# Layer 0 query projection as seven block products, rotated block by block, with the modulation weights loaded in halves

## The chip, the core and the metric

The kernel runs on one core of a Trainium2 chip. A core has five engines with a queue each: TensorE (PE; its weight loads are listed apart as PEld), VectorE (DVE), ScalarE (ACT), GpSimd (POOL) and SyncE (SP), which issues the DMA transfers. An engine works its own queue off in order and waits for the others at semaphores. The metric is the device time of one execution in microseconds (us), the median of several runs.

## The reference

Two transformer layers over x of 2 batches x 512 tokens x 512 features, all in fp32. Each layer has a modulated layer norm, attention, and a feed-forward part. The change touches only the attention of layer 0 and the products that make the modulation vectors:

```python
mod = (_silu(L0_c) @ L0_wmod).reshape(L0_c.shape[0], 6, 1, -1)   # 512 x 3072 weights, 2 rows
sa, ca, ga, sb, cb, gb = (mod[:, 0], mod[:, 1], ..., mod[:, 5])
h = _layernorm(x, axis=-1) * (1 + ca) + sa
# attention of layer 0: 32 query heads of 128, 8 key/value heads, window of 128 tokens
q = (x @ wq).reshape(B, S, 32, 128)      # x is h here; wq is 512 x 4096
k = (x @ wk).reshape(B, S, 8, 128)
v = (x @ wv).reshape(B, S, 8, 128)
q = _rope(q, pos); k = _rope(k, pos)     # [t1*cos - t2*sin, t1*sin + t2*cos] over the head's two halves
scores = einsum('bqhgd,bshd->bhgqs', qg, k) * 128 ** -0.5
allowed = (j <= i) & (j > i - 128)
attn = softmax(where(allowed, scores, min), axis=-1)
out = einsum('bhgqs,bshd->bqhgd', attn, v).reshape(B, S, 4096)
x = x + ga * (out @ wo)
```

## The kernel before

**Units and steps.** Layer 0's attention (`attention0`) works in 16 units: unit u is one key/value head (a group of 4 query heads) with one batch, the two batches of a group one after the other, so that even units bring in a new group of weights. A unit has four steps, one for each block `qb` of 128 queries; step n = 4u + qb. All tiles are transposed: features on the 128 partitions, tokens along the free dimension. The loop (under `tc.manual_schedule`, L965) writes out by hand the order in which PE, DVE, ACT and POOL get their instructions: the order of the program text is the order of each engine's queue. SP's order is set by a scheduler.

In step n of unit u, with `new` = u + 1, the text has in this order:

- `scores(u, qb)`: 4 or 8 small products into the one score tile in PSUM (`sp`, a single buffer), then on DVE the band mask (L809) and the row maximum (L815).
- The projections of the next unit: `keys(new)` and head 0 of the queries at qb 0, `values(new)` and head 1 at qb 1, heads 2 and 3 at qb 2 and 3.
- `turned`: the transposes of the step before (L844), their copies by ACT and DVE (L846).
- `exponentials` (ACT, reading `sp`; L825) and `normalised` (DVE reciprocal L834, POOL multiply L835).
- `product(u - 1, ...)`: the output projection of the unit before. It already is a seven-product (Strassen) form: each product is 4 matmuls of 256 columns (L903), added by DVE into sums that stay in SBUF (L911). The order is 1,2 / 7,4 / 5,6 / 3 over the four steps.
- `mix`: probabilities times values (L855), copied out by DVE (L862).
- `combine_rows` (L884, four POOL operations after the last `mix` of a unit), `combine_group` (L696, four POOL operations at the end of an even unit), and pieces of the modulation (`aside`).

**The query projection before.** `queries(u, hh)` calls `roped` (L736) for one head: 4 matmuls of 512 columns (the 512 features in 4 chunks, L740; the trace shows each fp32 matmul as two records) into one PSUM tile, then the rotation: three DVE multiplications that read that PSUM tile and the cosine/sine table (L745, L748, L749), and one POOL addition into `qT` (L750). All four heads of a unit are finished within the four steps before the unit's own first step.

**Buffers.** The PSUM pool `pmm` has four buffers, which keys, queries, values, products and mixes use in turn. The probabilities `p` have three buffers.

**Modulation.** Ten of the twelve 512 x 512 blocks of the modulation weights come in during the attention, in five pairs: a step issues the pair's two loads of 1 MB (`loads`, L558), the next one does its 8 matmuls (`mod_rows`, L99), the next turns the rows into columns or gates, and one pair has a `spread` step. The first pair (for the first norm) is loaded at the start.

**Feed-forward weights.** `Ffn0.loads` puts W and the low-rank matrices into the two buffers that the modulation weights used, from step 20 on.

Of the kernel before, what the change touches and what calls it, by code (L numbers as in the profile page):

```python
# [45 lines left out]
def adaln_kernel(ctx: ExitStack, tc: tile.TileContext, A: dict, out: bass.AP):  # L46
# [23 lines left out]
    def load_wmod(L, pool, bufs):  # L70

        src = A[f"L{L}_wmod"].rearrange("(kc p) n -> p kc n", p=P)

        def load(s):
            w = pool.tile([P, KC, D], F32, tag="wmod", name=f"wmod{L}_{s}", bufs=bufs)
            nc.sync.dma_start(out=w, in_=src[:, :, s * D : (s + 1) * D])
            return w

        return load
# [19 lines left out]
    def mod_rows(L, ws, sc, pool, tmp):  # L99

        n = 32 * len(ws)
        which = "".join(str(s) for s in ws)
        ps = pool.tile([P, 512], F32, tag="mm", name=f"psr{L}_{which}")
        for kc in range(KC):
            for i, w in enumerate(ws.values()):
                nc.tensor.matmul(
                    ps[32 * i : 32 * (i + 1), :],
                    lhsT=sc[:, kc, :],
                    rhs=w[:, kc, :],
                    start=(kc == 0),  # L110
                    stop=(kc == KC - 1),
                )
        rows = tmp.tile([P, D], F32, tag="rows", name=f"rows{L}_{which}", bufs=2)
        nc.scalar.copy(rows[:n, :], ps[:n, :])
        return rows
# [94 lines left out]
    class Ffn0:  # L210
# [3 lines left out]
        def __init__(self, gate, mid, wmp, ap, psum):  # L214
            self.gate, self.mid, self.wmp, self.ap, self.psum = gate, mid, wmp, ap, psum

        def loads(self):
            self.wT = self.wmp.tile([P, KC, D], F32, tag="wmod", name="wT0", bufs=2)
            nc.sync.dma_start(out=self.wT, in_=A["L0_ffn_WT"].rearrange("(kc p) o -> p kc o", p=P))

            self.ab = self.wmp.tile([P, KC, D], F32, tag="wmod", name="abT0", bufs=2)
            nc.sync.dma_start(
                out=self.ab[:, :, : 2 * P], in_=A["L0_ffn_AT"].rearrange("(kc p) e -> p kc e", p=P)
            )
            for j in range(2):
                nc.sync.dma_start(
                    out=self.ab[:, 2 * j : 2 * j + 2, 2 * P :],
                    in_=A["L0_ffn_BT"][j * P : (j + 1) * P, :].rearrange("p (h o) -> p h o", h=2),
                )
            co = self.mid.tile([P, 2, 2], F32, tag="co", name="co0")  # L230
            for i, n in enumerate(("L0_ffn_coeffs", "L0_ffn_scales")):
                for j in range(2):
                    src = A[n][j * 8 : (j + 1) * 8].unsqueeze(1).to_broadcast([8, R]).unsqueeze(2)
                    nc.sync.dma_start(out=co[:, i, j : j + 1], in_=src)
            self.wrow = self.mid.tile([P, 2], F32, tag="wrow", name="wrow0")
            nc.vector.tensor_mul(self.wrow, co[:, 0, :], co[:, 1, :])
# [30 lines left out]
        def tile(self, t):  # L267
            b, cols = t // TB, bass.ts(t % TB, P)
            ps = self.psum.tile([P, 512], F32, tag="mm", name=f"psf0_{t}")
            for kc in range(KC):  # L270
                nc.tensor.matmul(  # L271
                    ps, lhsT=hT[b][:, kc, cols], rhs=self.wT[:, kc, :], start=(kc == 0), stop=False
                )
            for j in range(2):
                nc.tensor.matmul(
                    ps.rearrange("p (h o) -> p h o", h=2),
                    lhsT=self.xa[:, 2 * b + j, cols],
                    rhs=self.ab[:, 2 * j : 2 * j + 2, 2 * P :],
                    start=False,
                    stop=(j == 1),  # L280
                )
            y = self.ap.tile([P, D], F32, tag="y", name=f"yf0_{t}", bufs=2)
            nc.vector.tensor_mul(y, ps, self.gate[b])
            nc.gpsimd.tensor_add(xs[t], xs[t], y)
# [247 lines left out]
    with ExitStack() as c01:  # L532
# [7 lines left out]
        with ExitStack() as c00:  # L540
            tables, load_group, combine_group = weights0(tc, A, c00)
            wmp = c00.enter_context(tc.tile_pool(name="wm", bufs=1))
            load = [load_wmod(L, wmp, 2) for L in range(2)]
            w = {s: load[0](s) for s in (0, 1)}
            load_x()
            tabs, groups = tables(), [load_group(0)]
            with ExitStack() as c0:
                pmm = c0.enter_context(tc.tile_pool(name="pmm0", bufs=3, space=PSUM))
                mod_columns(0, w, mod_rows(0, w, scs[0], pmm, wmp), pmm)
                norm = Norm(0, 0, 1, mid)  # L550
                for b in range(B):
                    norm.batch(b, pmm)

            def modulation(L, pair, pool):
# [3 lines left out]
                def loads():  # L558
                    held["w"] = {s: load[L](s) for s in pair}

                def rows():
                    held["r"] = mod_rows(L, held["w"], scs[L], pool, wmp)

                def rest():
                    if pair == (2, 5):
                        gate_rows(L, pair, held["r"], wmp, grow[L])
                    else:
                        mod_columns(L, pair, held["r"], pool)
# [4 lines left out]
                return [loads, rows, rest] + ([spread] if pair == (2, 5) and L == 0 else [])  # L573

            def finale(ap, pool):

                f = Ffn0(gate[5], mid, wmp, ap, pool)
                n0 = Norm(0, 3, 4, mid)
                end = (NKV * B - 2) * TB
                steps = {20: [f.loads]}  # L580
# [5 lines left out]
                steps[end + 5].insert(0, f.bias)  # L586

# [34 lines left out]
            def reload(t):  # L622
# [5 lines left out]
                tc, small, hT, xs, X, reload, gate[2], ident, tabs, groups, load_group,  # L628
                combine_group,
                lambda pool: [  # L630
                    f
                    for L, pair in ((0, (2, 5)), (0, (3, 4)), (1, (0, 1)), (1, (3, 4)), (1, (2, 5)))
                    for f in modulation(L, pair, pool)
# [21 lines left out]
def weights0(tc, A, ctx):  # L655
# [19 lines left out]
    def load_group(g):  # L675
# [7 lines left out]
        nc.sync.dma_start(out=w["q"], in_=wq[:, :, g * QW : (g + 1) * QW])  # L683
        for k in range(2):
# [10 lines left out]

    def combine_group(g, w):  # L696
# [9 lines left out]
    return tables, load_group, combine_group  # L706


def attention0(
    tc, small, hT, xs, X, reload, ga, ident, tabs, groups, load_group, combine_group, aside, finale  # L710
# [12 lines left out]
    with ExitStack() as ctx:  # L723
# [5 lines left out]
        kTs, vs, qTs, oTs, nms, pes, pTs, s3s, olds = ({} for _ in range(9))  # L729
# [6 lines left out]
        def roped(dst, wcols, b, name):  # L736

            ps = pmm.tile([P, 512], F32, tag="mm", name=f"ps_{name}")
            for kc in range(KC):
                nc.tensor.matmul(  # L740
                    ps, lhsT=wcols(kc), rhs=hT[b][:, kc, :], start=(kc == 0), stop=(kc == KC - 1)
                )
            co, si = rope[:, 0, :], rope[:, 1, :]
            t1 = ap.tile([P, S], F32, tag="t1", name=f"t1_{name}")
            nc.vector.tensor_mul(t1, ps, co)  # L745
            t2 = ap.tile([P, S], F32, tag="t2", name=f"t2_{name}")
            h = HD // 2
            nc.vector.tensor_mul(t2[:h, :], ps[h:, :], si[h:, :])  # L748
            nc.vector.tensor_mul(t2[h:, :], ps[:h, :], si[:h, :])  # L749
            nc.gpsimd.tensor_add(dst, t1, t2)  # L750

        def keys(u):
            g, b = units[u]
            kTs[u] = ap.tile([P, S], F32, tag="kT", name=f"kT{u}")
            roped(kTs[u], lambda kc: groups[g]["k"][:, kc, :], b, f"k{u}")
# [16 lines left out]
        def queries(u, hh):  # L772
            g, b = units[u]
            if hh == 0:
                qTs[u] = ap.tile([P, GRP, S], F32, tag="qT", name=f"qT{u}")
            roped(
                qTs[u][:, hh, :],
                lambda kc: groups[g]["q"][:, kc, hh * HD : (hh + 1) * HD],
                b, f"q{u}_{hh}",
            )  # L780

# [4 lines left out]
        def scores(u, qb):  # L786
# [4 lines left out]
            for hh in range(GRP) if qb == 0 else ():  # L791
                nc.tensor.matmul(
                    sp[:, hh, o:],
                    lhsT=qTs[u][:, hh, :P],
# [4 lines left out]
            for hh in range(GRP) if qb else ():  # L799
                for h in range(2):  # L800
# [3 lines left out]
                        lhsT=qTs[u][:, hh, qb * P + h * H2 : qb * P + (h + 1) * H2],  # L804
# [13 lines left out]
        def exponentials(u, qb):  # L818
# [3 lines left out]
            pe = ap.tile([P, GRP, 2 * P], F32, tag="p", name=f"p{u}_{qb}", bufs=3)  # L822
# [61 lines left out]
        def combine_rows(u):  # L884

            a11, a12, a21, a22 = quarters(u)
            s3 = s3s[u] = ap.tile([P, 2, DH], F32, tag="s3", name=f"s3_{u}", bufs=1)
            nc.gpsimd.tensor_sub(s3, a11, a21)
            nc.gpsimd.tensor_add(a21, a21, a22)
            nc.gpsimd.tensor_sub(a11, a21, a11)  # L890
            nc.gpsimd.tensor_sub(a12, a12, a11)
# [45 lines left out]
        def output(u, i):  # L937
# [12 lines left out]
            y = ap.tile([P, D], F32, tag="y", name=f"ya{u}_{i}", bufs=2)  # L950
# [3 lines left out]
        aside = aside(pmm)  # L954
# [10 lines left out]
        with tc.manual_schedule(engines=FOUR):  # L965
            for n in range(-TB, NU * TB + 2):
# [6 lines left out]
                if new < NU:  # L973
                    if qb == 0:
                        keys(new)
                        queries(new, 0)
                    elif qb == 1:
                        values(new)
                        queries(new, 1)
                    else:  # L980
                        queries(new, qb)
# [8 lines left out]
                if 0 <= u - 1 < plain:  # L990
                    for i in ((1, 2), (7, 4), (5, 6), (3,))[qb]:
                        product(u - 1, i)
                if 0 <= n - 1 < NU * TB:
                    mix(*before)
                    if before[1] == TB - 1 and before[0] < plain:
                        combine_rows(before[0])
                for f in filling.get(n, ()):
                    f()
                if 0 <= u < plain and qb == TB - 1 and units[u][1] == 0:
                    combine_group(units[u][0], groups[units[u][0]])  # L1000
                for f in regaining.get(n, ()):
# [792 lines left out]
```

## Time and profile before

Three runs took 2500.97 us (median), 2496.91 and 2504.66. The profiled execution took 2495.89 us; its span, from first to last instruction, is 2494.0 us. The rest, 1.9 us, lies around the span.

| what | value |
|---|---|
| span of the profiled execution | 2494.0 us |
| time of the profiled execution | 2495.89 us |
| median of three runs | 2500.97 us |
| PE busy, whole span | 2425.6 us (97%) |
| attention of layer 0, unit 0's first scores to the last group's end | about 60 to 845 us of the span |
| one unit in the steady part (scores of qb 0 to the next scores of qb 0) | 545.06 to 592.80 us: 47.74 us |
| mean granted TensorE clock over the span | 0.985 |

Two notes for reading. In a timeline row the columns are: start, time from the first instruction's start to the last one's end, engine, line, operation, out<-in, partitions x elements, count, and in brackets the idle time of the engine before it and what ended it. PE's instructions are pipelined and their ends are modelled, so the time that a set of matmuls costs is read from its start to the start of the next set.

### The profile page before, as it was taken

The numbers are of one execution on the slowest core, as the hardware profiler recorded it, in microseconds if no ns is written. First come the engines' busy times: TensorE is split into PE (matmuls) and PEld (weight loads), VectorE is DVE, ScalarE is ACT, GpSimd is POOL, SyncE is SP. The second block draws the span as 40 slices with busy tenths as digits, with TensorE's granted clock in tenths as the row PEclk, the third lists the DMA queues.
The fourth block names the chain that finished last, engine by engine and source line by source line (L and its number), as shares of the span: only waits on it lengthen the run. The fifth ranks groups of instructions, "written<-read, shape, count | busy, mean of one in ns | idle before, by whom it ended". The sixth has DMA issues, their size and how long they took to land.

```text
span 2494.0 us, 30184 instructions
## 1 busy us (share of the span) xinstructions
PE 2425.6 (97%) x11036; PEld 1196.2 (48%) x11036; DVE 1719.7 (69%) x2352; ACT 1411.4 (57%) x2106; POOL 1634.9 (66%) x1563
## 2 busy tenths in 40 slices
PE   7999999999999999999999999999999999999878
PEld 3566666666666544444444344444344444444333
DVE  4546666655667436788777788778777877788764
ACT  1222212212222116888888888878788888888650
POOL 1434444344356414888888988889888888888743
PEclk8999999999999999999999999999999999999988
DMA  6221100100000101000000000000000000110000
GB/s 231 79 74 60 43 14 30 41 15 30 13 6 29 32 15 34 26 26 19 25 26 26 22 26 26 26 26 18 30 26 26 26 18 26 30 29 22 18 9 34
DMA packets 74559, 83.06 MB, mean 33 GB/s; under 512 B 7725, under 2 KB 58700, under 8 KB 74412
## 3 DMA queue, kind: packets, MB, share of 16 engines
q1 hardware_dynamic: 74268, 81.00, 10.3%
q8 instruction: 87, 1.43, 0.2%
q14 instruction: 60, 0.49, 0.1%
q0 software_dynamic: 144, 0.15, 0.0%
HBM read 79.03 MB, written 2.10 MB: 33 GB/s over the span
## 4 chain that ended last, share of the span: by engine, by line
PE 94%; DVE 4%; ACT 1%; DMA 0%; issue 0%; POOL 0%; SPq 0%; DVEq 0%; ACTq 0%; POOLq 0%
PE s L1247 19%; PE psq L1180 18%; PE acc L1402 10%; PE ps_q L740 9%; PE pw L903 7%; PE s L1256 5%; PE po L855 4%; PE scores L802 3%; PE psv L762 2%; PE ps_k L740 2%; PE pt L844 2%; PE psu L1199 2%; PE psm L1326 2%; PE psw L1458 1%; PE psf L506 1%; PE psf L271 1%
## 5 line engine op out<-in xcount | busy, mean ns | idle before, releaser
L1353 POOL TENSOR_TENSOR ss<-ss,row 128x512 f32<-128x512 f32 x504 | 635.2, 1288 | 41.6 <-ACT row L1338 41.6
L1266 ACT COPY ss<-s 128x1024 f32<-128x1024 f32 x512 | 505.7, 1015 | 177.7 <-PE s L1256 130.6
L1247 PE MATMUL s<-q,ckr 64*128 64x512 f32 x2048 | 554.7, 612 | 10.5 <-ACT ss L1266 10.5
L1356 ACT ACTIVATE ss<-ss 128x1024 f32<-128x1024 f32 x512 | 525.2, 1070 | 5.6 <-DVE ss L1568 4.5
L1180 PE MATMUL psq<-hT,wqr 128*128 128x512 f32 x1024 | 467.2, 598 | 0.0
L1256 PE MATMUL s<-qm,c 64*128 64x512 f32 x1024 | 419.1, 794 | 0.4 <-DVE c L1217 0.4
L1273 DVE TENSOR_TENSOR mx<-s,mx 128x1024 f32<-128x1024 f32 x256 | 306.5, 1218 | 40.1 <-PE s L1256 39.1
L1347 POOL TENSOR_TENSOR ss<-ss,rowe 128x512 f32<-128x512 f32 x252 | 318.2, 1286 | 0.0
L1180 PEld LDWEIGHTS psq<-hT,wqr 128*128 128x128 f32 x1024 | 188.9, 189 | 241.0 <-issue 210.4
L750 POOL TENSOR_TENSOR qT<-t_q,t_q 128x512 f32<-128x512 f32 x64 | 81.6, 1274 | 331.4 <-DVE t_q L749 331.4
L1247 PEld LDWEIGHTS s<-q,ckr 64*128 64x128 f32 x2048 | 184.2, 186 | 215.1 <-ACT ss L1266 99.1
L846 ACT COPY pT<-pt 128x512 f32<-128x512 f32 x64 | 37.5, 586 | 426.4 <-PE pt L844 426.4
L1402 PE MATMUL acc<-ss,vp 128*32 128x512 f32 x2048 | 265.1, 611 | 0.0
L1273 DVE TENSOR_TENSOR mx<-s,ss 128x1024 f32<-128x1024 f32 x128 | 156.8, 1225 | 118.0 <-ACT row L1338 80.1
L740 PE MATMUL ps_q<-hT,wq 128*128 128x512 f32 x512 | 233.3, 598 | 0.0
L1256 PEld LDWEIGHTS s<-qm,c 64*128 64x128 f32 x1024 | 104.5, 187 | 119.0 <-issue 114.9
L1278 DVE STREAM_TRANSPOSE mx<-mx 128x1024 f32<-128x1024 f32 x128 | 158.6, 1239 | 2.3
L1316 POOL TENSOR_TENSOR st<-mh,own_block 128x512 fp32r<-128x512 f32 x64 | 67.1, 1048 | 141.8 <-DVE mh L1312 141.8
L1284 DVE TENSOR_REDUCE m<-mx 128x32 f32<-128x1024 f32 x128 | 156.1, 1219 | 4.4
L1349 DVE TENSOR_TENSOR ss<-ss,psm 128x512 f32<-128x512 f32 x252 | 155.7, 679 | 0.0
L740 PEld LDWEIGHTS ps_q<-hT,wq 128*128 128x128 f32 x512 | 93.5, 190 | 109.2 <-issue 108.6
L745 DVE TENSOR_TENSOR t_q<-ps_q,rope 128x512 f32<-128x512 f32 x64 | 44.3, 691 | 133.2 <-PE ps_q L740 131.8
(235 smaller groups left out, 3480.2 us busy)
## 6 DMA issues: line engine op xcount, KB each, us to landing
wqr<-in_L_attn_Wq_rope_pairs SPq DMA_DIRECT2D x64, 512.0 KB
wmod<-in_L_wmod SPq DMA_DIRECT2D x12, 1024.0 KB
wq<-in_L_attn_wq SPq DMA_DIRECT2D x8, 1024.0 KB
wo<-in_L_attn_wo SPq DMA_DIRECT2D x32, 256.0 KB
x<-in_L_attn_x SPq DMA_DIRECT2D x8, 256.0 KB
wk<-in_L_attn_wk SPq DMA_DIRECT2D x8, 256.0 KB
wv<-in_L_attn_wv SPq DMA_DIRECT2D x8, 256.0 KB
xi<-in_L_attn_x SPq DMA_DIRECT2D x8, 256.0 KB
```

Source lines behind the costliest of these rows:

```text
L740: nc.tensor.matmul(ps, lhsT=wcols(kc), rhs=hT[b][:, kc, :], start=(kc == 0), stop=(kc == KC - 1))
L903: nc.tensor.matmul(ps[:, j, :], lhsT=s[:, hh, j * P : (j + 1) * P], rhs=t[:, hh, :], start=(hh == 0), stop=(hh == 1),)
L1180: nc.tensor.matmul(ps, lhsT=wqs[t][:, kc, pair * P : (pair + 1) * P], rhs=hT[b][:, kc, :], start=(kc == 0), stop=(kc == KC - 1),)
L1247: nc.tensor.matmul(out[:, j, :], lhsT=whole[b]["kr"][r, bass.ts(i, P)], rhs=qs[t, p][r, :], start=True, stop=False,)
L1256: nc.tensor.matmul(out[:, j, :], lhsT=qkc[t // 2, 1][r, bass.ts(i, P)], rhs=qm[t, p][r, :], start=False, stop=True,)
L1266: nc.scalar.copy(ss[t, i, p], hold["s", t, i, p])
L1273: nc.vector.tensor_max(mx[t, p], hold["s", t, i, p], before)
L1278: nc.vector.transpose(m, m)
L1347: nc.gpsimd.tensor_sub(s, s, hold["r", t, 2])
L1353: nc.gpsimd.tensor_sub(s, s, hold["r", t, 2 * p + 1])
L1356: nc.scalar.activation(ss[t, i, p], ss[t, i, p], AF.Exp)
L1402: nc.tensor.matmul(accs[g, b][32 * h : 32 * (h + 1), :], lhsT=vps[t][:, kb, h, :], rhs=ss[t, kb, h // 2][:, h % 2, :], start=(s == 0 and k ...
```

## The change

**Seven products.** Within a unit the query projection is a product of a 512 x 512 weight block (4 heads x 128) with 512 x 512 tokens. It is cut into 2 x 2 blocks (heads 0-1 and 2-3; features 0-255 and 256-511; tokens 0-255 and 256-511) and done as seven block products of 4 matmuls with 256 columns each, in place of 4 heads x 4 matmuls with 512 columns. `queries(u, i)` does product i; the sums are made in the blocks of the result, `q11, q12, q21, q22`, which lie in SBUF (`qT`): product 1 is copied there by ACT, the others are added by DVE from PSUM.

**Sums of operands.** New function `combine_queries` makes four sums of weight blocks on POOL (three, then one), once for each group; new function `combine_tokens` makes four sums of token blocks on POOL, once for each unit.

**Rotation by block.** A block of the result (2 heads x 256 tokens) is rotated when its last product has been added: `roped` now reads the block from SBUF, three DVE multiplications and one POOL addition into the block. `q11` is complete after product 2, `q21` after 4, `q22` after 5, `q12` after 3.

**Places.** Products 1 / 2 / 6,7 / 4 of the next unit stand at qb 0 / 1 / 2 / 3; products 5 and 3 follow in the unit's own steps qb 0 and 1 (`queries(u, (5, 3)[qb])`), ahead of the transposes. The products of the output projection are spread as 1,2 / 7 / 6,4 / 5,3, and `combine_rows` over three steps.

**Memory.** `p` has two buffers for three; the output rows `y` share the tag of `t1`.

**Modulation in halves.** The ten later blocks are loaded in halves of 256 columns, two tiles at a time; a step does the first half's products and then issues the second half's loads, so that a pair takes four steps for three. The first pair is loaded whole as before, and its rows are made in two halves. `Ffn0`'s weights go into the buffers of the query weights, at steps 56 and 61.

```diff
-        ps = pool.tile([P, 512], F32, tag="mm", name=f"psr{L}_{which}")
+        ps = pool.tile([P, 512], F32, tag="mm", name=f"psr{L}_{which}{h}")
...
-                    ps[32 * i : 32 * (i + 1), :],
+                    ps[32 * i : 32 * (i + 1), :DH],
...
+                def turn():
+                    rows(0)
+                    loads(1)
...
-                return [loads, rows, rest] + ([spread] if pair == (2, 5) and L == 0 else [])
+                return [lambda: loads(0), turn, lambda: rows(1), rest] + ends
...
-                steps = {20: [f.loads]}
+                steps = {end: [f.loads]}
...
+    def combine_queries(g, w, k):
+        a11, a12, a21, a22 = w["quarters"]
+        part = lambda i: wp.tile([P, 2, DH], F32, tag="sq", name=f"s{i}_{g}", bufs=3)
+        if k == 0:
+            s3, s2 = part(3), part(2)
+            nc.gpsimd.tensor_sub(s3, a11, a21)
+            nc.gpsimd.tensor_add(a21, a21, a22)
+            nc.gpsimd.tensor_sub(s2, a21, a11)
+            w["s"] |= {5: a21, 6: s2, 7: s3}
+        else:
+            w["s"][3] = s4 = part(4)
+            nc.gpsimd.tensor_sub(s4, a12, w["s"][6])
...
-            nc.vector.tensor_mul(t1, ps, co)
-            nc.vector.tensor_mul(t2[:h, :], ps[h:, :], si[h:, :])
-            nc.vector.tensor_mul(t2[h:, :], ps[:h, :], si[:h, :])
+            nc.vector.tensor_mul(t1, src, table(0, whole))
+            nc.vector.tensor_mul(t2[lo], src[up], table(1, up))
+            nc.vector.tensor_mul(t2[up], src[lo], table(1, lo))
             nc.gpsimd.tensor_add(dst, t1, t2)
...
+        def combine_tokens(u):
+            b11, b12, b21, b22 = tokens(units[u][1])
+            t3, t1, t2, t4 = (
+                ap.tile([P, 2, DH], F32, tag="th", name=f"th{i}_{u}", bufs=4) for i in (3, 1, 2, 4)
+            )
+            nc.gpsimd.tensor_sub(t3, b22, b12)
+            nc.gpsimd.tensor_sub(t1, b12, b11)
+            nc.gpsimd.tensor_sub(t2, b22, t1)
+            nc.gpsimd.tensor_sub(t4, b21, t2)
+            ths[u] = {4: t4, 5: t1, 6: t2, 7: t3}
...
+            s = groups[g]["s"][i]
+            t = tokens(b)[{1: 0, 2: 2, 3: 3}[i]] if i < 4 else ths[u][i]
+            ps = pmm.tile([P, 2, DH], F32, tag="mm", name=f"ps_q{u}_{i}")
+            for j in range(2):
+                for k in range(2):
+                    nc.tensor.matmul(ps[:, j, :], lhsT=s[:, k, j * P : (j + 1) * P],
+                                     rhs=t[:, k, :], start=(k == 0), stop=(k == 1))
+            if i == 1:
+                nc.scalar.copy(q12, ps)
+            for to, of in {
+                2: ((q11, q12),), 6: ((q12, q12),), 7: ((q22, q12),), 4: ((q21, q22),),
+                5: ((q12, q12), (q22, q22)), 3: ((q12, q12),),
+            }.get(i, ()):
+                nc.vector.tensor_add(to, of, ps)
+            done = {2: (q11, 0), 4: (q21, 0), 5: (q22, 1), 3: (q12, 1)}.get(i)
+            if done:
+                q, n = done
+                roped(q, q, slice(n * DH, (n + 1) * DH), f"q{u}_{i}")
...
-                        queries(new, 0)
...
-                        queries(new, 1)
-                    else:
-                        queries(new, qb)
+                    for i in ((1,), (2,), (6, 7), (4,))[qb]:
+                        queries(new, i)
+                if 0 <= u < NU and qb < 2:
+                    queries(u, (5, 3)[qb])
...
-                    for i in ((1, 2), (7, 4), (5, 6), (3,))[qb]:
+                    for i in ((1, 2), (7,), (6, 4), (5, 3))[qb]:
                         product(u - 1, i)
                 if 0 <= n - 1 < NU * TB:
                     mix(*before)
-                    if before[1] == TB - 1 and before[0] < plain:
-                        combine_rows(before[0])
+                if 0 <= u - 1 < plain and qb < 3:
+                    combine_rows(u - 1, qb)
...
+                if new < NU and qb == 0:
+                    combine_tokens(new)
+                if new < NU and units[new][1] == 0 and 0 <= qb - (new > 0) < 2:
+                    combine_queries(units[new][0], groups[units[new][0]], qb - (new > 0))
```

## The prediction

> **What bounds the kernel now.** I read the chain of waits first.
>
> ```profile
> PE 94%; DVE 4%; ACT 1%; DMA 0%; issue 0%; POOL 0%; SPq 0%; DVEq 0%; ACTq 0%; POOLq 0%
> ```
>
> TensorE sets the time. The busy times by stretch (columns: PE, PEld, DVE, ACT, POOL, granted clock, DMA share, GB/s) say the same of layer 0's steady part: PE has no idle time, POOL works 45%, DVE 60%.
>
> ```profile
> 500.00:600.00 100.00, 100.00 (x464) 64.34 (x463) 59.89 (x85) 20.22 (x75) 45.06 (x34) 1.00 0.09 27
> ```
>
> Those are means. What decides is who waits for whom within a step, so I read one unit (545.06 to 592.80, 47.74 us) in the timeline, here its step qb 1:
>
> ```profile
> 558.96 1.52 PE L802 MATMUL scores<-kT,qT 128*64 128x192 f32 x16
> 560.41 3.84 PE L762 MATMUL psv<-wv,hT 128*128 128x128 f32 x32
> 564.09 3.60 PE L740 MATMUL ps_q<-hT,wq 128*128 128x512 f32 x8
> 567.52 0.60 PE L844 MATMUL pt<-ident,p 128*128 128x128 f32 x4
> 567.96 1.89 PE L903 MATMUL pw<-t,s 128*128 128x256 f32 x8
> 569.69 1.89 PE L903 MATMUL pw<-t,oT 128*128 128x256 f32 x8
> 571.42 1.02 PE L855 MATMUL po<-pT,v 128*128 128x512 f32 x2
> 572.37 1.52 PE L802 MATMUL scores<-kT,qT 128*64 128x192 f32 x16
> ```
>
> From start to start: scores 1.45, values 3.68, one head 3.43, transposes 0.44, one product of 256 columns 1.73, mix 0.95. What follows a head on the other engines:
>
> ```profile
> 567.80 0.69 DVE L745 TENSOR_TENSOR t_q<-ps_q,rope 128x512 f32<-128x512 f32 x1 [4.77 <-PE ps_q L740]
> 568.50 0.69 DVE L748 TENSOR_TENSOR t_q<-ps_q,rope 64x512 f32<-64x512 f32 x1
> 569.20 0.68 DVE L749 TENSOR_TENSOR t_q<-ps_q,rope 64x512 f32<-64x512 f32 x1
> ...
> 569.97 1.27 POOL L750 TENSOR_TENSOR qT<-t_q,t_q 128x512 f32<-128x512 f32 x1 [4.81 <-DVE t_q L749]
> 571.20 1.89 POOL L835 TENSOR_TENSOR p<-p,rs 128x1024 f32<-128x1024 f32 x1
> ```
>
> DVE starts 0.28 us after PE's next start, takes 0.70 us an operation; POOL follows 0.1 us later and takes 1.27 us, 1.35 from start to start where one sum needs the last (559.84 to 561.19, L888 and L889). Before, this had steps to spare: the heads of unit u+1 are ready before that unit's first scores.
>
> **The saving.** A unit's four heads cost 3.43 + 3.43 + 3.54 + 3.54 = 13.94 us; the two at qb 2 and 3 (573.82 to 577.36 and 584.95 to 588.49) run a little longer. Seven products at the L903 row's 1.73 cost 12.11. So 1.83 us a unit, 29 us over 16 units. That row is the same form (4 matmuls, 256 columns) with its weight loads hidden; I take it as it is.
>
> **The new wait of every unit.** Blocks q22 and q12 are finished in the unit's own steps: product 5 at qb 0, product 3 at qb 1. `scores(u, 2)` at the next step reads q12. Count from the start of step qb 1. PE: scores 1.45, values to 5.13, product 2 to 6.86, product 3 to 8.59, transposes, one product (7) and mix to 11.71; then it wants scores. DVE: product 2's sum at 6.86 + 0.28 = 7.14, then three rotations, 4 x 0.70, to 9.94; product 3's sum to 10.64. POOL adds q11 from 10.04 to 11.31. The next rotation has both inputs in SBUF, where POOL reads. Rows for this:
>
> ```profile
> 750.64 2.36 DVE L934 TENSOR_TENSOR x<-x,g 128x512 f32<-128x512 f32 x2
> 750.80 1.65 POOL L888 TENSOR_TENSOR s<-oT 128x512 f32<-128x512 f32 x1 [2.37 <-DVE oT L862]
> ```
>
> Two such operations took 2.36 in place of 1.4, and POOL's 1.65 in place of 1.27 (L934 alone runs from 0.68 to 1.76). So it waits for POOL's end: 11.31, three rotations to 13.4, POOL's sum of q12 from 13.5 to 14.8, scores at 14.9: a wait of 3.2 us. Without that collision all moves 0.67 earlier: 2.5. Even with empty queues 0.28 + 0.70 + 2.10 + 0.10 + 1.27 = 4.45 stand against the 3.12 that PE has between product 3 and scores: 1.3. I take 3.2.
>
> [...]
>
> **The second new wait, in odd units** (7 times, u = 1, 3 .. 13, where the next unit brings a group). Product 6 at qb 2 reads s2, the third sum of `combine_queries`. In POOL's queue that stands behind q12 (14.8), the softmax multiply (1.85, to 16.6), two `combine_rows` (2 x 1.35, to 19.3), then three sums (to 23.4). PE, let go at 14.9, has done its scores at 16.35: a wait of 7.1 us. Nothing in these sums is off POOL's path, so I see no lower price than 6.5 and no higher than 8 (rows L888 to L891 range from 1.27 to 1.65).
>
> **What lies beside other work, at no cost.** `combine_tokens`: POOL idles between the last row sum of qb 0 and q11 above; its four sums end at 7.7 in that step, just ahead of the first rotation (9.9 us after the step began q11 needs POOL). Seven sums on DVE (5 us a unit) and ACT's copy (0.59): DVE then has 34 us of 46; what of it is late is in the wait above. The four PSUM buffers: the closest reuse, product 6 of the output after 7, leaves over 6 us. Two buffers of `p`: a buffer is free once transposed, a step before ACT needs it. q21 (product 4 at qb 3): DVE has it rotated 7.1 and POOL 8.4 after the step's start, PE wants it at 9.2; 0.8 of cover. Modulation: the same columns on PE (3.56 us a pair before); ACT copies twice, idle 78%. The second half's load (1 MB) has a step of some 10 us; at the start 2 MB landed within 8 us of issue. On SP's queue it waits for the first half's matmuls, and behind it stand weights due many steps later. If that cover is gone, PE waits a few us five times: 15 at worst.
>
> **The ends.** Start: product 6 of unit 0 needs eight sums behind POOL's first (34.2 us; 3.4 of wait), q21 then 4.6 of wait; scores 0 come at 58.3 for 60.5, but the spread's 3.4 us (54.04 on) are still to do, and unit 0's own wait is 5 us (it has no output products as cover) less 1.83 and less some of the 2.6 that it idles now: together +4 (-3 to +10). Last unit: product 5 lands in it (1.73) and q12 comes about 2.2 late: +4 (2 to 6).
>
> **The clock.** After a wait of 2.12 us the trace shows half speed:
>
> ```profile
> 54.04 6.54 PE L145 MATMUL psg<-grow,ident 64*128 64x512 f32 x8 [2.12 <-DVE grow L136]
> ```
>
> The stretch from there, with the columns of the table above (0.53 is the clock):
>
> ```profile
> 54.00:65.00 11.00, 10.96 (x20) 5.08 (x21) 3.36 (x5) 3.22 (x5) 1.26 (x1) 0.53 0.00 0
> ```
>
> Eight records of 0.43 took 6.54; the clock stayed at 0.53 for some 10 us. A wait of 1.77 (805.89) was followed by full speed. So 2 us decide, and the new waits lie above. Price of one: between nothing and half of those 10 us, 5.1. At 826 us the slow stretch after such waits is shorter, some 5 us after work resumes, a loss of 2.6: I take 2.6 for each odd unit (wait nearly 10 us in two parts) and 1.2 for the others (3.2 is close to the edge). 7 x 2.6 + 8 x 1.2 = 28 (0 to 50).
>
> [...]
>
> **Sum.** Units 1 to 14: 14 x (3.2 - 1.83) = 19; odd ones 7 x 7.1 = 50; ends 8; clock 28: +105 us. The profiled execution would take 2495.9 + 105 = 2601; the median of runs lies 5 above that execution: 2501 + 105 = 2606.
>
> **Rivals.**
> - The clock holds: the waits alone, +77, 2578 (2560 with the lower bounds of waits and start). For it: 1.77 left no trace. Against: 2.12 did, and 7.1 is far above. 22%.
> - The clock falls for 10 us at all 15 places: 15 x 5.1 = 77 for 28, 2655. For it: the one clean row. Against: that row's matmuls use half the array's rows, which may be why it stayed low. 9%.
> - Faster: the waits are hidden. All turns on POOL and DVE in step qb 1: two units save 3.66, so their waits (now 3.2 + 3.2 + 7.1) must come to less than that. With empty queues 1.3 each remains: 16 x (1.83 - 1.3) = 8, 2493; with no wait at all 29, 2472. For it: POOL is busy only 45% now and the sums' results may be wanted later than I read. Against: the order of queues is fixed, and even 1.3 needs POOL free. 6%.
> - The seven products don't run as seven: PE's queue shows 28 matmuls of 256 columns a unit. Other causes of about no change: 3%. Other, slower: 5%.
>
> **How the numbers follow.** The forecast (2606, its own range 2580 to 2640) has 55%. The range reaches down to the clock's rival, 2558, and up to 2640 by the upper clock bound (2501 + 77 + 50 + the ends' 8). A measurement of this kernel can't tell 0.3% (7.5 us) from no change: faster 6%, same 3%, slower 91%.
>
> **What would show it.** In the changed profile: scores waiting for POOL's qT some 3 us a unit; ps_q waiting for POOL's s some 7 us seven times; units of 49 us alternating with 56 and more; granted clock below 1 in 120 to 900 us, where it is 1.00 now. Units near 46 us, or the wait for s missing, would prove me wrong; a clock of 1.00 would take away the 28.

## The result and the profile after

| | before | after |
|---|---|---|
| median of four runs each, side by side | 2500.02 us | 2604.27 us |
| profiled execution (its span) | 2495.89 us (2494.0) | 2603.92 us (2601.9) |
| mean granted TensorE clock | 0.985 | 0.966 |
| unit 1 begins | 103.75 us | 109.03 us |
| unit 15 begins | 790.67 us | 895.09 us |
| first product of the feed-forward (`psf`) | 848.89 us | 957.28 us |

The ratio is 1.0416, 95% interval 1.0398 to 1.0434: slower by 104 us. The profiled executions lie 108 us apart, and the table says where: 104.4 us are there when unit 15 begins and 4 more when the feed-forward begins, so all of it is in layer 0's attention.

In the page of the changed kernel, the chain of waits:

```profile
PE 86%; DVE 8%; POOL 3%; issue 1%; ACT 1%; DMA 0%; SPq 0%; DVEq 0%; POOLq 0%; ACTq 0%
```

TensorE's share has fallen from 94 to 86%, DVE's has risen by 4 and POOL's by 3. These are shares of the chain of work that ended last, not the size of the loss; the size stands in the view of what TensorE waited for (who waited, for whom, us in total, times, longest):

```profile
PE scores L891 <- POOL qT L786: 50.4, 16, 5.7
PE ps_q L849 <- POOL s L722: 47.8, 8, 6.8
...
PE psr L103 <- DMA wmod<-in_L_wmod: 7.6, 2, 6.9
...
PE scores L881 <- POOL qT L786: 4.1, 1, 4.1
```

The two named waits are new: 16 and 8 times, 98 us together. The wait for modulation weights is as long as before (7.7 us then). One odd unit's steps qb 1 and 2 in the timeline of TensorE:

```profile
461.18 1.52 PE L891 MATMUL scores<-kT,qT 128*64 128x192 f32 x16
...
468.03 1.89 PE L849 MATMUL ps_q<-hT,s 128*128 128x256 f32 x8
...
475.82 2.01 PE L891 MATMUL scores<-kT,qT 128*64 128x192 f32 x16 [2.87 <-POOL qT L786]
484.13 6.78 PE L849 MATMUL ps_q<-th,s 128*128 128x256 f32 x16 [6.30 <-POOL s L722]
490.74 1.04 PE L933 MATMUL pt<-ident,p 128*128 128x128 f32 x8
```

and POOL's queue in the same stretch, in the columns of the timeline:

```profile
471.20 1.28 POOL L786 TENSOR_TENSOR qT<-t_q,t_q 128x512 f32<-128x512 f32 x1 [2.72 <-DVE t_q L785]
474.50 1.26 POOL L786 TENSOR_TENSOR qT<-t_q,t_q 128x512 f32<-128x512 f32 x1 [2.03 <-DVE t_q L785]
475.73 1.89 POOL L924 TENSOR_TENSOR p<-p,rs 128x1024 f32<-128x1024 f32 x1
477.58 1.26 POOL L980 TENSOR_TENSOR oT<-oT 128x512 f32<-128x512 f32 x1
478.92 1.26 POOL L981 TENSOR_TENSOR oT<-oT 128x512 f32<-128x512 f32 x1
480.13 1.26 POOL L720 TENSOR_TENSOR s<-wq 128x512 f32<-128x512 f32 x1
481.47 1.26 POOL L721 TENSOR_TENSOR wq<-wq 128x512 f32<-128x512 f32 x1
482.81 1.26 POOL L722 TENSOR_TENSOR s<-wq 128x512 f32<-128x512 f32 x1
```

Read them against each other. The second L786 row is q12: it ends at 475.76, and 0.06 us later TensorE starts the scores. The last row is s2: it ends at 484.07, and 0.06 us later product 6 starts. Between them POOL is never idle for as much as 0.1 us. The work behind the waits is slow as well: products 6 and 7 take 6.61 us (484.13 to 490.74) where two products at the forecast's price take 3.46.

Stretches of an odd and an even unit (columns as in the prediction; the clock is the third from the end):

```profile
447.26:506.21 58.95, 49.78 (x251) 38.06 (x250) 33.56 (x48) 10.44 (x38) 32.92 (x26) 0.88 0.07 22
506.21:556.84 50.63, 47.77 (x252) 36.62 (x251) 33.46 (x48) 10.96 (x39) 22.93 (x18) 0.97 0.09 28
```

58.95 and 50.63 us stand for 47.74 before, at a clock of 0.88 and 0.97 for 1.00. POOL works 33 and 23 us of them: it is late, not full. How low the clock falls shows in the middle of the odd unit's products 6 and 7, in the same columns:

```profile
484.00:490.00 6.00, 5.87 (x14) 4.71 (x15) 0.69 (x1) 0.00 (x0) 0.08 (x1) 0.50 0.00 0
```

### The profile page after: what moved, and what is told of

Its sections match the earlier page's. It is cut to its first block, busy times and chain, and to the rows that moved or that the text cites. A ratio compares the mean times of both kernels' runs of the same rounds, so it can differ in the third digit from the quotient of the medians.

```text
span 2601.9 us, 31431 instructions
## 1 busy us (share of the span) xinstructions
PE 2436.1 (94%) x11516; PEld 1297.5 (50%) x11516; DVE 1804.3 (69%) x2464; ACT 1421.4 (55%) x2128; POOL 1756.2 (67%) x1659
## 4 chain that ended last, share of the span: by engine, by line
PE 86%; DVE 8%; POOL 3%; issue 1%; ACT 1%; DMA 0%; SPq 0%; DVEq 0%; POOLq 0%; ACTq 0%
PE s L1343 18%; PE psq L1276 17%; PE acc L1498 9%; PE ps_q L849 7%; PE pw L995 5%; PE s L1352 5%; PE po L944 3%; PE scores L891 2%; PE ps_k L793 2%; PE psv L807 2%; PE psu L1295 2%; PE pt L933 1%; PE psm L1422 1%; PE psw L1554 1%; DVE t_q L783 1%; PE psf L505 1%
## 5 line engine op out<-in xcount | busy, mean ns | idle before, releaser
L786 POOL TENSOR_TENSOR qT<-t_q,t_q 128x512 f32<-128x512 f32 x64 | 81.9, 1280 | 230.7 <-DVE t_q L785 230.7
L924 POOL TENSOR_TENSOR p<-p,rs 128x512 f32<-128x512 f32 (+1 forms) x64 | 108.6, 1696 | 113.7 <-DVE rs L923 110.1
L862 DVE TENSOR_TENSOR qT<-qT,ps_q 128x512 f32<-128x512 f32 x112 | 75.3, 684 | 147.3 <-PE ps_q L849 146.8
L1335 POOL TENSOR_SCALAR qm<-c,cols 128x512 fp32r<-128x512 f32 x64 | 102.6, 1603 | 44.0 <-PE s L1352 24.7
```

## The experiments

Seven kernels, each beside runs of the kernel before on the same chip. The unit lengths below go from one unit's first scores to the next one's.

### Which wait costs what: each undone alone, then both

The first gives the sums of the query weights a unit's time (`load_queries` is the query part of `load_group`, cut out of it):

```diff
+ if 0 <= u < NU and qb == 0 and units[u][1] == 0 and units[u][0] + 1 < NKV:
+     load_queries(units[u][0] + 1)
...
- if new < NU and units[new][1] == 0 and 0 <= qb - (new > 0) < 2:
-     combine_queries(units[new][0], groups[units[new][0]], qb - (new > 0))
+ if new == 0 and qb < 2:
+     combine_queries(0, groups[0], qb)
+ if 0 <= u < NU and qb == 2:
+     g, b = units[u]
+     if b == 0 and g + 1 < NKV:
+         combine_queries(g + 1, ahead[g + 1], 0)
+     elif b == 1 and g + 1 < NKV:
+         combine_queries(g + 1, groups[g + 1], 1)
```

> Edit: the query weights of the next group are loaded at qb 0 of the even unit, and the three sums that make s3, a21+a22 and s2 are issued at qb 2 of that unit, one unit before product 6 reads them; the order on TensorE is unchanged. Theory (product 6 waits 6.3 us in 7 odd units because s2 stands at the end of POOL's queue of the same step, and that idle time brings the half-speed stretch): the wait before product 6 goes, and with it about 3.1 us of clock loss an odd unit, while the 2.9 us before scores at qb 2 stay: 2604 - 7 x 9.4 = 2538 us (2530 to 2550). Rival 1 (POOL is short of time, the sums only push its other work later): the 27 us of POOL work moved into even units come out as new waits there, 2580 to 2604. Rival 2 (the clock loss belongs to the wait before scores): only the waits go, 2604 - 44 = 2560.

Measured: 2550.52 us, 1.0203 (1.0188 to 1.0219) of the kernel before; 53.8 below the changed kernel. The one wait left for `s` is that of the start (6.0 us). Odd units in the middle fall from 58.8 to 49.0 or 50.7, even ones stay at 50.7 (one falls to 49.0): POOL had room for the moved sums, so the first rival falls, and the 53.8 exceed the second's 44, the waits alone. The expected 66 were not reached: a pair of units gained 8.6 us from unit 5 to 12 and 6.9 from unit 1 to 4, where 9.4 were counted. The waits that went were 41.8 us, not 44, and the wait that is left goes on costing clock:

```profile
357.46 1.52 PE L899 MATMUL scores<-kT,qT 128*64 128x192 f32 x16 [2.88 <-POOL qT L794]
406.49 2.55 PE L899 MATMUL scores<-kT,qT 128*64 128x192 f32 x16 [2.87 <-POOL qT L794]
457.16 2.03 PE L899 MATMUL scores<-kT,qT 128*64 128x192 f32 x16 [2.87 <-POOL qT L794]
```

That is the timeline of this kernel, the scores of three units: the same work after the same wait, slow in two and at full speed in one. Its units 11 and 12, each with one such wait, in the stretch table (clock 0.97 and 1.00):

```profile
629.66:680.34 50.68, 47.80 (x251) 36.79 (x250) 33.56 (x48) 10.44 (x38) 29.20 (x23) 0.97 0.08 26
680.34:729.30 48.96, 46.09 (x251) 35.73 (x250) 33.46 (x48) 10.96 (x39) 26.63 (x21) 1.00 0.07 18
```

The second moves products 5 and 3 on TensorE:

```diff
  if 0 <= u < NU:
      scores(u, qb)
+ if 0 <= u < NU and qb < 2:
+     queries(u, (5, 3)[qb])
  if new < NU:
      if qb == 0:
          keys(new)
...
- if 0 <= u < NU and qb < 2:
-     queries(u, (5, 3)[qb])
```

> Edit: products 5 and 3 of a unit come right after its scores on TensorE, ahead of keys, values and products 1 and 2 of the next unit; nothing else is moved. Theory (q12 comes out of POOL too late because product 3 lies behind values and product 2): product 3 runs 5.4 us earlier, so the wait before scores at qb 2 goes in every unit. In the odd units the sum s2 leaves POOL when it did, so product 6 waits for as much longer (6.3 + 2.9 = about 9) and they stay at 59 us. Even units lose the wait and its clock loss, 50.6 to about 46.5 us: 2604 - 8 x 4 = 2572 us (2560 to 2585). Rival 1 (each wait is a cost by itself): the odd units gain too, 2604 - 15 x 3.5 = 2552. Rival 2 (the wait is POOL's load, not the place of product 3): q11 or q21 is late in place of q12 and the time stays at 2595 to 2610.

Measured: 2569.34 us, 1.0276 (1.0259 to 1.0293). Even units take 46.65 us, 4.0 less, with no wait before scores. Odd ones from unit 5 to 11 keep 56.4 to 57.8, and their wait has moved as the theory said, in the timeline:

```profile
459.64 1.52 PE L891 MATMUL scores<-kT,qT 128*64 128x192 f32 x16
469.76 5.25 PE L849 MATMUL ps_q<-th,s 128*128 128x256 f32 x16 [8.60 <-POOL s L722]
```

8.60 in one piece for 2.87 and 6.30 in two. So the waits are not costs by themselves: in an odd unit POOL's chain from q11 to s2 sets the time, and taking away the first wait lengthens the second. These odd units still gain some 1.6 us on average, 0.5 of it in the waits and 0.5 in products 6 and 7, which take 5.7 us to the next start behind the one wait and 6.2 behind the two; the rest no run explains.

Both edits together:

> Both edits: query-weight sums one unit earlier, products 5 and 3 right after the scores. Theory (these two waits and the clock that they cost are all that stands between the change and its saving in the steady part): no wait left in units 1 to 14, clock 1.00, a pair of units 2 x (47.74 - 1.83) = 91.8 us in place of 109.6: 2604 - 7 x 17.8 = 2480 us (2470 to 2490), below the kernel before by about 20, the start still some 5 us late. Rival (Strassen's extra sums do not fit POOL and DVE, a product costs more than 1.73): waits turn up elsewhere and the time stays above 2500.

Measured: 2495.54 us, 0.9983 (0.9973 to 0.9992), 108.7 below the changed kernel. From unit 5 to 12 the units take 46.65 us at a clock of 1.00, odd and even alike, so these two waits and their clock were the loss. But 46.65 is 0.74 above the expected 45.91, and 2495.54 lies outside the expected range. The timeline of a steady unit:

```profile
448.52 1.89 PE L857 MATMUL ps_q<-th,wq 128*128 128x256 f32 x8
450.25 3.60 PE L801 MATMUL ps_k<-hT,wk 128*128 128x512 f32 x8
...
463.00 1.99 PE L857 MATMUL ps_q<-hT,s 128*128 128x256 f32 x8
464.83 3.73 PE L815 MATMUL psv<-wv,hT 128*128 128x128 f32 x32
...
474.79 3.72 PE L857 MATMUL ps_q<-th,s 128*128 128x256 f32 x16
478.34 1.04 PE L941 MATMUL pt<-ident,p 128*128 128x128 f32 x8
479.56 3.72 PE L1003 MATMUL pw<-t,oT 128*128 128x256 f32 x16 [0.18 <-POOL oT L989]
```

From start to start, product 5 takes 1.73 us, product 3 takes 1.83, products 6 and 7 take 3.55; with 1.73, 1.73 (products 1 and 2) and 1.83 (product 4) the seven make 12.40. And the transposes after product 7 take 1.22 to the next start for 0.87 in other steps: product 6 of the output waits there for a row sum of POOL. Together that is 0.64 of the 0.74.

### What the clock costs

Matmuls whose results nobody reads fill the two gaps: `busy` is called in `queries`, ahead of product 6, and in the loop, ahead of the scores of qb 2.

```diff
+            if i == 6 and b == 0 and u:
+                busy(ps.rearrange("p h n -> p (h n)"), 7)
...
+        def busy(out, times):
+            for _ in range(times):
+                nc.tensor.matmul(out, lhsT=ident, rhs=hT[0][:, 0, :], start=True, stop=True)
...
+                    if qb == 2:
+                        early[u, 1] = pst.tile([P, GRP, P], F32, tag="t", name=f"pt{u}_1_0")
+                        busy(early[u, 1].rearrange("p h n -> p (h n)"), 3)
                     scores(u, qb)
```

> Edit: the changed kernel with matmuls added whose results nobody reads: three of 512 columns before scores at qb 2 of each unit (into the buffer that the transposes overwrite) and seven before product 6 in the odd units (into its own block, which it overwrites). At the 0.86 us that a 512-column matmul takes, they fill 2.6 of the 2.9 us and 6.0 of the 6.3 us that TensorE waits; POOL and DVE have the same work. Theory (the idle time itself halves the clock, and the slow stretch costs 3.7 us an odd and 1.7 us an even unit): the waits' length stays in the time, the clock stays at 1.00 there, 2604 - 7 x 3.7 - 8 x 1.7 = 2564 us (2555 to 2575). Rival 1 (the slow stretch is not the idle time's doing, or does not cost what the rows seem to say): 2600 to 2610. Rival 2 (the added matmuls come in the way of the real ones): above 2610.

Measured: 2581.61 us, 1.0329 (1.0313 to 1.0344): 22.7 below the changed kernel though TensorE does more. In the timeline of an odd unit TensorE now idles 0.30 and 0.61 us where it idled 2.87 and 6.30:

```profile
464.95 2.74 PE L874 MATMUL pt<-hT,ident 128*128 128x512 f32 x6
467.99 1.52 PE L899 MATMUL scores<-kT,qT 128*64 128x192 f32 x16 [0.30 <-POOL qT L786]
469.44 6.28 PE L874 MATMUL ps_q<-hT,ident 128*128 128x512 f32 x14
476.32 3.72 PE L851 MATMUL ps_q<-th,s 128*128 128x256 f32 x16 [0.61 <-POOL s L722]
479.88 1.04 PE L943 MATMUL pt<-ident,p 128*128 128x128 f32 x8
```

Scores take 1.45 to the next start again, products 6 and 7 take 3.56, and the stretch table has the clock at 1.00:

```profile
420.00:530.00 110.00, 108.80 (x557) 80.61 (x554) 70.77 (x101) 21.79 (x78) 59.16 (x45) 1.00 0.08 25
```

Odd units take 55.9 us for 58.8, even ones 49.0 for 50.6. So it is the idle time that halves the clock (0.50 in products 6 and 7 of the changed kernel, 1.00 here), and that costs 22.7 us of the 104; the expected 40 were too many. In an odd unit the slow scores cost nothing, as POOL sets the start of product 6: it starts 8.33 us after the scores' start here, 8.31 in the changed kernel. And in the changed kernel some even units had no loss at all: unit 6 takes 49.03, the length with the clock held.

### The rest of the change, without the seven products

The edit puts the projection by heads back into the changed kernel:

```diff
- for i in ((1,), (2,), (6, 7), (4,))[qb]:
-     queries(new, i)
- if 0 <= u < NU and qb < 2:
-     queries(u, (5, 3)[qb])
+ queries(new, qb)
...
- if new < NU and qb == 0:
-     combine_tokens(new)
```

> Edit: the changed kernel with the query projection of the kernel before (four heads of 512 columns, rotation from the product, no sums of tokens or query weights); what stays of the change is the modulation weights in halves, the moved loads of layer 0's feed-forward, two softmax buffers for three, the shared buffer of the output rows and the row sums in three steps. Theory (all of that lies beside other work, as the prediction priced it): 2500 us, within 4. Rival (the second half's load or the scarcer buffers hold TensorE up, up to 15 us): 2505 to 2515, with waits at psr, at the softmax or at the output rows that the kernel before does not have.

Measured: 2499.46 us, 0.9999 (0.9991 to 1.0008). The halves, the shared buffers, the two softmax buffers and the split row sums cost nothing that can be measured in the whole. In this run's profile, though, unit 1 begins 2.0 us later than before (105.70), units 1 to 4 take 1.7 us more and the last unit 1.5, so that the feed-forward begins 5.1 us later (854.03); what follows it takes 3.0 us less, which no run explains.

### The two ends

```diff
  with tc.manual_schedule(engines=FOUR):
+     combine_queries(0, groups[0], 0)
      for n in range(-TB, NU * TB + 2):
...
-     if new == 0 and qb < 2:
-         combine_queries(0, groups[0], qb)
+     if new == 0 and qb == 0:
+         combine_queries(0, groups[0], 1)
```

> Edit: the kernel with both earlier edits (2495.5 us), and the first group's three sums of query weights issued ahead of the loop, where POOL idles until 33 us; its fourth sum a step earlier. Theory (the start is late because product 6 of unit 0 waits 6.0 us behind five other sums on POOL, and the idle time costs some clock too): that wait goes, 2495.5 - 6 - 2 = 2487 us (2484 to 2491). Rival (the rotation of q21 at the end of the start is what scores 0 wait for, whatever product 6 does): its wait of 4.1 grows to 10 and the time stays at 2494 to 2496.

Measured: 2486.74 us, 0.9954 (0.9941 to 0.9968): faster than both kernels, and as expected. The wait of product 6 in unit 0 is gone, and unit 0's scores begin at 49.71 us, for 55.71 in the kernel with both edits. That kernel's wait, and then the scores of this one:

```profile
45.53 6.56 PE L857 MATMUL ps_q<-th,s 128*128 128x256 f32 x16 [6.01 <-POOL s L729]
```

```profile
49.71 0.61 PE L889 MATMUL scores<-kT,qT 128*128 128x128 f32 x4
```

In its timeline two waits of over 2 us are left from unit 1 to the end of unit 15, both for q12, in units 14 and 15:

```profile
750.85 1.52 PE L899 MATMUL scores<-kT,qT 128*64 128x192 f32 x16 [3.44 <-POOL qT L794]
...
798.22 1.52 PE L899 MATMUL scores<-kT,qT 128*64 128x192 f32 x16 [2.09 <-POOL qT L794]
```

The last kernel goes for the one in unit 14 and for the 4.1 us ahead of unit 0's scores:

```diff
- regaining.setdefault(n + TB + k, []).append(lambda b=b, k=k: residual(b, k))
+ regaining.setdefault(n + TB + 1 + k, []).append(lambda b=b, k=k: residual(b, k))
...
- if aside and n >= -3:
+ if aside and n >= -2:
```

> Edit: the one with the early start, and besides the residual sums of each batch one step later (out of the step in which product 3's block is rotated in unit 14) and the pieces of the modulation one step later (so that one half's matmuls stand between product 4 and the first scores). Theory (POOL's and DVE's other work in unit 14 makes q12 late there by 3.5 us, and the start's last wait of 4.1 us has nothing of TensorE's beside it): 3.5 and about 1 of clock from unit 14, 1.9 from the start, 2487 - 6.4 = 2481 us (2477 to 2486). Rival (what moves out of these steps holds up the next ones: the softmax of unit 14 at qb 2, the norm's statistics): 2487 or more.

Measured: 2486.20 us, 0.9946 (0.9933 to 0.9958), no different from the run with the early start (2486.74). The expected gain did not come, and the rival's account held, with the time 0.8 us below its bound. Unit 14 fell from 56.51 us to 53.29 and has no wait for q12, and the 4.1 us ahead of unit 0's scores went; but the modulation's half then waited 2.7 us for its DMA, and the norm at the end waits for the sums that were moved towards it, in this kernel's timeline:

```profile
815.87 0.30 PE L185 MATMUL pst<-ident,xn 128*128 128x128 f32 x1 [2.93 <-DVE xn L176]
```

1.98 in the kernel without these moves. Unit 15 begins 3.9 us earlier, its feed-forward 1.2.

## Why the prediction was right

The forecast was 2606 us by two new waits, the clock and the ends; the measured 2604 came about in that way. That it was met within 2 us is partly luck, as the terms show:

| term | predicted | measured |
|---|---|---|
| saving of a unit | 1.83 us | 1.58 in unit 6, which kept its clock; 1.09 with both edits |
| scores at qb 2 wait for q12 | 3.2 us | 2.87 in most units |
| product 6 waits for s2, odd units | 7.1 us | 5.5 to 6.8 idle, 41.8 in all (47.8 less 6.0 at the start); 6.8 at full clock |
| clock | 28 us | 22.7, from the run with the clock held: odd units 1.8 to 3.0, even ones about 0 to 1.6 |
| start and unit 0 | +4 | +5.3: unit 1 begins at 109.03, before at 103.75; product 6 waits 6.0 there for 3.4 forecast, q21's scores 4.1 for 4.6 |
| last unit | +4 | +4.0: 62.19 us from its scores to `psf`, 58.22 before |
| halves and buffers | 0 | 0 (0.9999, 0.9991 to 1.0008) |

**The chain in step qb 1** held row by row. Counted from the step's start at 461.18 (predicted times in brackets): q11 leaves POOL at 11.30 (11.31), q12's rotation ends at 13.25 (13.4), q12 leaves POOL at 14.58 (14.8), s2 at 22.89 (23.4). TensorE wanted its scores at 11.77 (11.71). The differences add up from one or two tenths a row, to 0.5 at s2.

**The collision** is there, though smaller than forecast, and no run here takes it away. DVE in that step:

```profile
471.15 0.69 DVE L862 TENSOR_TENSOR qT<-qT,ps_q 128x512 f32<-128x512 f32 x1
471.94 1.08 DVE L783 TENSOR_TENSOR t_q<-qT,rope 128x512 f32<-128x512 f32 x1
473.04 0.69 DVE L784 TENSOR_TENSOR t_q<-qT,rope 64x512 f32<-64x512 f32 x1
```

The first multiplication of q12 takes 1.08 us for 0.69 and ends 0.54 us after POOL's sum of q11 (472.48): 0.39 us lost, where the forecast took 0.67. So the wait of 2.87 lies between the 3.2 taken and the 2.5 without a collision. The row agrees in kind with the forecast's L934, where two such operations took 2.36 us for 1.4 and ended 0.55 us after POOL's sum (753.00 and 752.45); the forecast had the multiplication end its own 0.69 after the sum, not 0.54.

**The saving** was mis-sized. Unit 6 of the changed kernel, whose clock stayed at 1.00, in the stretch table and in the timeline:

```profile
398.24:447.26 49.02, 46.16 (x252) 35.72 (x251) 33.45 (x48) 10.96 (x39) 22.89 (x18) 1.00 0.10 29
```

```profile
428.23 3.72 PE L849 MATMUL ps_q<-th,s 128*128 128x256 f32 x16
431.79 1.04 PE L933 MATMUL pt<-ident,p 128*128 128x128 f32 x8
432.66 3.62 PE L995 MATMUL pw<-t,oT 128*128 128x256 f32 x16
...
439.38 1.99 PE L849 MATMUL ps_q<-th,wq 128*128 128x256 f32 x8
441.21 1.04 PE L933 MATMUL pt<-ident,p 128*128 128x128 f32 x8
```

Without its wait of 2.86 the unit takes 46.16, so 1.58 us are saved of the 1.83. Products 6 and 7 take 3.56 from start to start and product 4 takes 1.83; with the others at 1.73 the seven make 12.3, not 12.11. The row taken for the price was a product of the output projection; why these three cost more, no run shows. The 1.09 of the kernel with both edits has the wait of the output's product for its row sum in it, which the changed kernel does not have: its transposes there take 0.87 (431.79 to 432.66).

**The sum.** Units 1 to 14 together cost 99 us more (97 forecast). The waits for q12 make 44.7 (50.4 less 3.65 in unit 0 and 2.09 in unit 15; unit 14 alone has 5.7). In every odd unit product 6 starts 8.31 us after the scores do; in unit 5, where these ran at full speed, 6.79 of it is idle, so the wait for s2 is 7 x 6.79 = 47.5 with the clock at full. With 22.7 of clock, and less 14 x 1.58, that is 93. Some 6 us stay unassigned; 1.7 of them may be those that units 1 to 4 take more with the halves alone. Of the forecast's clock, the 1.2 us for an even unit, whose wait of 3.2 us it put close to an edge, was the author's estimate: no run shows an edge there, and behind waits of 2.86 to 2.88 us units lost from about 0 to 1.6. Against the forecast, the waits for s2 came out 2 us smaller and the clock 5; the saving came out 3.5 us smaller, the ends 1 us larger, and there are the 6. That these nearly cancel is luck; the two waits, their places and the fall of the clock are not.

**The rivals.** Clock at full: 2578 forecast; the run with the clock held gave 2582, so that path was priced about right, and it is not what happens. Clock down for 10 us at all places: units would have lost 5 us each, 2655; they lost 0 to 3.0. That half of the array's rows kept the one clean row slow was a guess, which no run tested. Waits hidden: 2493 with 1.3 us left of each, 2472 with none; in this kernel they were not hidden. An order that hides them gave 2495.5, and 2486.7 with the start mended. The products did run as seven: the timeline has each at 8 records, for 4 matmuls.

## What to carry to other kernels

- A saving on the engine that sets the time is only had if what it adds on the others is ready before that engine asks. Count from the step's start in each queue, product by product; the busy share of the helper (here POOL at 33 of 59 us) says nothing of it.
- Two waits on one queue can be one cost: removing the first moved the wait to the second (2.87 + 6.30 became 8.60), while removing the second left the first as it was. Work whose inputs have long been there (sums of weights) belongs a whole stage earlier, and the product whose result has the longest way to go comes first in its step: these two moves turned 1.042 of the time before into 0.998, and the start's sums ahead of the loop made it 0.995.
- Idle time of the engine that sets the time can cost more than itself: here some 23 us of lowered clock on top of it. Useless matmuls in the gap show how much, though they can't remove the gap.

## What the runs showed of the hardware

- Idle times of 2.87 us lowered the clock, but not each of them. In the run with only that wait left (the sums early), eight units had it at 2.87 or 2.88 us between 357 and 709 us; five of these units took 50.7 us, those with the waits' ends at 357.46, 558.51 and 708.90 took 49.0. The clock was 0.97 in the unit from 629.66 us and 1.00 in the one from 680.34, each with a wait of 2.88. What sorts the slow ones from the fast, no run shows.
- Where a rotation's multiplication on VectorE, with both inputs in SBUF, met a running GpSimd sum, it ended 0.54 or 0.55 us after that sum: it took 1.08 us above for its own 0.69, and 1.74 and 1.67 in the kernel with product 3 moved, where two of them met the sums of the tokens. The sum that started meanwhile took 1.60 for 1.27. Over a unit this is small; ahead of a block that TensorE waits for, it lengthens the wait (0.39 us above).
